# Router scores by GpSimd products and halving sums, and the choice of experts one sequence into the next tile

## The chip, the cores and the metric

The kernel runs on one core of a Trainium2 chip. A core has a matrix engine (TensorE, PE in the profile), VectorE (DVE), ScalarE (ACT), GpSimd (POOL), a queue engine that only issues transfers (SyncE, SP) and 16 DMA engines. Each engine works through its own queue in order and waits there for what its next instruction needs. The metric is the device time of one launch in microseconds (us), median of several runs; lower is better.

## The reference

One transformer block in float32: `x` is 64 sequences of 32 tokens of width 256, and each sequence has a context of 257 rows of width 128.

```python
x = x + cross_attention(layernorm(x), ctx)      # 16 heads of 64, keys and values from ctx
x = x + self_attention(layernorm(x))            # 4 heads of 64, half of each head with rotary angles
x = x + mixture_of_experts(layernorm(x))        # 8 experts, 2 per token
```

The part that matters here is the router of the last line. With `x` now the normed rows and `Wr` of 8 x 256:

```python
scores = einsum('bsd,nd->bsn', x, Wr) + br                 # 8 numbers per token
w      = softmax(scores)
_, idx = top_k(scores + biases_N, 2)                       # two experts per token
val    = take_along_axis(w, idx); val = val / val.sum(-1)
```

Each expert is `silu(x@Wl1_a + bl1_a) * (x@Wl1_b + bl1_b)`, 256 to 512, followed by `@ Wl2 + bl2`, 512 to 256; a token's two results are added with the weights `val`.

## The kernel before

**Tiles.** The 2048 tokens are 16 tiles `t` of 128 tokens, four sequences `b` each. The main loop (L1037) runs over the 64 pairs `(t, b)`. A pass of it transposes the probabilities of sequence `(t, b)` on PE (`probs_transposed`, tile `tp`, L338), mixes the context with them (`cross_mix`, `pa`, L348), and meanwhile forms the scores of the *next* sequence (`cross_probs`: `s` on PE L315, the negated maximum `nmx` on VectorE L319, the exponential on ScalarE L320, `inv` on VectorE L325, and the scaling `pr` of the four groups of 128 rows in two pairs, VectorE L327). So the second L327 pair of one pass is what the third and fourth `tp` transpose of the next pass need.

**Work beside it.** All else of the attention part is in Python generators that the loop advances a unit at a time, by the table `steps` (L932): one row per sequence of an even and an odd tile, six places in a row. `"near"` is the generator `rest(t)` (L557) of the tile before the loop's own, `"far"` that of the tile two before, `"ahead"` the cross-attention queries of the next pair of tiles (`cross_queries`, L250), which start at the end of each odd tile. `rest(t)` has 13 units: the cross-attention's output and a layer norm (3), self-attention (7, the rotary products L407 to L412 among them), and from unit 11 on `route(t, xr)` (L475): unit 11 transposes the normed rows `xr` (`trr`, PE, copied by ScalarE to `xrT`); unit 12 multiplies `xrT` with `Wr` (`pr`, L483, a 128x8 result) and chooses the experts with a dozen small VectorE instructions (`rsc` L485 to `xr` L522); unit 13 turns the choice into row numbers (`pk` on PE L527, `rat` to `rslots`, `seen`) and writes the rows to the expert lists in DRAM with two indirect transfers from the POOL queue (`routed`, L539). `carry` (L555) is a POOL instruction that hands the counts to the next tile. A tile takes 6 near and 7 far units, so its two experts are chosen in the third row (`b` = 2) and its rows written in the fourth row of the far tile.

**Layer norms.** `normed` (L173) takes statistics on VectorE, one power (`rstd`, L183) on POOL, and the scaling on VectorE (L186); its results are `xns`, `xr` and `xnq`. VectorE stands in its queue while POOL makes the power.

**Who sets the order.** PE and SP issue in the order of the program (`manual_schedule`, L79). ScalarE, VectorE and POOL are put in an order by a planner, which moves an instruction ahead of others where its estimates let it; `cross_queries`, traced at the end of an odd tile, has its two norms run two sequences earlier. `tc.keep_in_program_order(i)` holds `i` behind the instruction that was traced last on its engine, and behind that one alone.

**The expert part.** At the start of tile 15 `early_blocks` (L760) counts the lists up to the last tile that has been routed and prepares 6 blocks of 128 rows; after the loop these and the blocks of `late_blocks` run, 28 of them in the profiled execution, PE-bound, with weights streamed by SP.

**Queues.** SP issues every load in program order: the first loads end with `bn_bc` (L155), then come the zeros for `routed` (L1014), the context of tile 1 and so on. POOL's queue holds the powers, two additions `xb` and `axb` of 128x256 per tile (L356, L467), `carried`, the `routed` transfers, and in the expert part the adding transfers to the output.

Of the kernel before, what the change touches and what calls it, by code (L numbers as in the profile page):

```python
# [9 lines left out]
FP = mybir.dt.float32  # L10
# [6 lines left out]
P = 128  # L17
# [33 lines left out]
def block_kernel(  # L51
# [13 lines left out]
    awo: bass.AP,  # L65
    abo: bass.AP,
    freq: bass.AP,
    wr_t: bass.AP,
    br: bass.AP,
    bias_n: bass.AP,  # L70
# [38 lines left out]
    def pool(name, bufs):  # L109
        return ctx.enter_context(tc.tile_pool(name=name, bufs=bufs))  # L110
# [55 lines left out]
    sm = pool("sm", 4)  # L166
    xp = pool("xp", 3)
    tb = pool("tb", 1)

    def bank(shape, name):  # L170
        return ps.tile([P] + shape, FP, tag="a", name=name)
# [17 lines left out]
    def transposed(dst, src, n, name, beside=False):  # L189


        if beside:
            pt = ps.tile([P, n, P], FP, tag="t", bufs=2, name=f"tr{name}")
        else:
            pt = bank([n, P], f"tr{name}")
        for k in range(n):
            nc.tensor.transpose(pt[:, k, :], src[:, k * P : (k + 1) * P], ident)
        nc.scalar.copy(dst, pt)  # L198
# [276 lines left out]
    def route(t, xr):  # L475

        nc.gpsimd.tensor_copy(xr[:, RW - 1 : RW], token[:, t : t + 1])
        xT = wk.tile([P, 2, P], FP, tag="xrT", name=f"xrT{t}")
        transposed(xT, xr, 2, f"r{t}", t < NT - 2)
        yield  # L480
        pr = bank([NE], f"pr{t}")
        for k in range(2):
            nc.tensor.matmul(pr, xT[:, k, :], wr_sb[:, k, :], start=(k == 0), stop=(k == 1))  # L483
        sc = sm.tile([P, NE], FP, tag="rsc", name=f"rsc{t}")
        nc.vector.tensor_tensor(sc, pr, br_bc, ALU.add)  # L485
        sel = sm.tile([P, NE], FP, tag="rsel", name=f"rsel{t}")
        nc.vector.tensor_tensor(sel, sc, bn_bc, ALU.add)
        top = sm.tile([P, 8], FP, tag="rtop", name=f"rtop{t}")
        nc.vector.max(top, sel)
        idx = sm.tile([P, 8], U32, tag="ridx", name=f"ridx{t}")  # L490
        nc.vector.max_index(idx, top, sel)
        idf = sm.tile([P, 2, 1], FP, tag="ridf", name=f"ridf{t}")
        nc.vector.tensor_copy(idf[:, :, 0], idx[:, 0:2])

        two = sm.tile([P, 2, NE], FP, tag="rtwo", name=f"rtwo{t}")
        nc.vector.tensor_tensor(
            two, expert_id2, idf.to_broadcast([P, 2, NE]), ALU.is_equal
        )
        both = sm.tile([P, NE], FP, tag="rboth", name=f"rboth{t}")
        nc.vector.tensor_tensor(both, two[:, 0, :], two[:, 1, :], ALU.add)  # L500
        boths[t] = both
        if t < NT - 2:


            fed = sm.tile([P, NE], FP, tag="rfed", name=f"rfed{t}")
            nc.vector.scalar_tensor_tensor(fed, both, not_last, carried[t], ALU.mult, ALU.add)
        nmx = sm.tile([P, 1], FP, tag="rnmx", name=f"rnmx{t}")
        nc.vector.tensor_reduce(nmx, sc, AX.X, ALU.max, negate=True)
        ex = sm.tile([P, NE], FP, tag="rex", name=f"rex{t}")
        if t < NT - 2:  # L510
            nc.scalar.activation(ex, sc, AF.Exp, bias=nmx)
        else:

            nc.vector.tensor_scalar(ex, sc, nmx, None, ALU.add)
            nc.gpsimd.tensor_tensor(ex, euler, ex, ALU.pow)
        nc.vector.tensor_tensor(ex, ex, both, ALU.mult)
        tot = sm.tile([P, 1], FP, tag="rtot", name=f"rtot{t}")
        nc.vector.tensor_reduce(tot, ex, AX.X, ALU.add)
        inv = sm.tile([P, 1], FP, tag="rinv", name=f"rinv{t}")
        nc.vector.reciprocal(inv, tot)  # L520
        ew = xr[:, D : D + NE]
        nc.vector.tensor_scalar(ew, ex, inv, None, ALU.mult)  # L522
        yield

        pk = bank([NE], f"pk{t}")
        if t < NT - 2:
            nc.tensor.matmul(pk, before_all, fed, start=True, stop=True)  # L527
        else:
            nc.tensor.matmul(pk, before, both, start=True, stop=False)
            nc.tensor.matmul(pk, of_last, seen[t - 1], start=False, stop=True)  # L530
        at = sm.tile([P, 1, NE], FP, tag="rat", name=f"rat{t}")
        nc.vector.tensor_tensor(at[:, 0, :], pk, region[:, 0, :], ALU.add)
        nc.vector.tensor_tensor(two, two, at.to_broadcast([P, 2, NE]), ALU.mult)
        slot = sm.tile([P, 2], FP, tag="rslot", name=f"rslot{t}")
        nc.vector.tensor_reduce(slot, two, AX.X, ALU.add)
        slots = sm.tile([P, 2], U32, tag="rslots", name=f"rslots{t}")
        nc.vector.tensor_copy(slots, slot)
        for k in range(2):
            nc.gpsimd.indirect_dma_start(  # L539
                out=routed[:, :],  # L540
                out_offset=bass.IndirectOffsetOnAxis(ap=slots[:, k : k + 1], axis=0),
                in_=xr,
                in_offset=None,
            )
        if t >= NT - 2:

            nc.gpsimd.dma_start(out=out[t * P : (t + 1) * P, :], in_=xs[t])
        if t < NT - 1:
            seen[t] = sm.tile([P, NE], FP, tag="seen", name=f"seen{t}")
            nc.vector.tensor_tensor(seen[t], pk, both, ALU.add)  # L550
            carry(t)
# [308 lines left out]
    def rotary_tables():  # L860
# [69 lines left out]


    steps = (  # L932
        ("", "far", "ahead", "near", "far", ""),
        ("near", "far", "", "near", "far", ""),
        ("ahead", "far", "ahead", "near", "far", "ahead"),
        ("near", "", "ahead", "near", "", "far"),
        ("", "far", "ahead", "near", "far", ""),
        ("near", "far", "", "near", "far", ""),
        ("ahead", "far", "ahead", "near", "far", "ahead"),
        ("", "", "near", "near", "", "far"),  # L940
    )
    last_steps = steps[4:6] + (
        ("", "", "far", "near", "", "far"),
# [1 line left out]
    )  # L945
    kvs, probs = {0: context0}, {}
    seqs = [(t, b) for t in range(NT) for b in range(4)]
    work = {"near": last_rows(), "far": iter(()), "ahead": cross_queries(0)}
    next(work["ahead"])

    diag = [const.tile([P, AH, P], FP, name=f"diag{i}") for i in range(2)]
# [85 lines left out]
    for n, (t, b) in enumerate(seqs):  # L1037
        if n == 1:
            work["ahead"] = cross_queries(1)
            next(work["ahead"])  # L1040
        if n == 2:
            next(work["ahead"])
        if n == 3:
            load(base, freq.partition_broadcast(P))
        if n == 5:
            rotary_tables()
        if t == NT - 1 and b == 0:
            blocks, done = early_blocks()
            lane_of_queries(0)
        if b == 0:  # L1050
            cT = wk.tile([P, XH, 4, SEQ], FP, tag="cT", name=f"cT{t}")
            lastT = wk.tile([P, 4, SEQ], FP, tag="lastT", name=f"lastT{t}")
            if t + 1 < NT:
                kvs[t + 1] = load_context(t + 1)
            if t % 2 == 0 and t + 4 < NT:
                for j in (t + 4, t + 5):
                    load_tokens(j)
        place = iter(steps[4 * (t % 2) + b] if t < NT - 1 else last_steps[b])

        def step():  # L1060
            name = next(place)
            if name:
                next(work[name], None)

        scores = iter(())
        if n + 1 < len(seqs):
            t1, b1 = seqs[n + 1]
            scores = cross_probs(t1, b1, kvs[t1][0])
        pr, pts = probs.pop((t, b)), []
        probs_transposed(t, b, 0, pr, pts)  # L1070
        step()
        next(scores, None)
        next(scores, None)
        step()
        probs_transposed(t, b, 1, pr, pts)
        nc.vector.transpose(lastT[:, b, :], p_last[t % 2][b])
        next(scores, None)
        step()
        next(scores, None)
        step()  # L1080
        step()
        cross_mix(t, b, pts, kvs[t][1], cT)
        step()
        if t == NT - 1 and b == 1:
            load_last(t)
            blocks.weights(0, (0, 1), sure=True)
            for i in range(EARLY - 1):
                blocks.gathered(i)
        if b == 3:
            if t < NT - 1:  # L1090
                load_last(t)
            if t % 2:
                for _ in work["ahead"]:
                    pass
                if t + 3 < NT:
                    work["ahead"] = cross_queries((t + 3) // 2)
                    next(work["ahead"])
            for _ in work["far"]:
                pass
            work["far"] = work["near"]  # L1100
            work["near"] = rest(t, cT, lastT, u_ring[t % 3])

# [144 lines left out]
```

## Time and profile before

| | |
|---|---|
| median of 3 runs | 801.58 us (800.68 to 804.30) |
| the profiled execution's own time | 802.53 us |
| its span in the trace | 800.8 us |
| attention part | from 0 to about 600 us |
| one tile of it in the steady state | about 36 us (the router transposes of tiles 5 and 7 start at 291.1 and 363.2 us) |
| busy: PE, VectorE, ScalarE, POOL | 96%, 63%, 46%, 19% |
| POOL additions of 128x256 (`axb`), one | 724 / 726 / 743 ns (min / median / max) |
| `pr` scaling L327, one | 334 / 350 / 834 ns |

The profile page gives busy times and groups; the trace behind it can be asked for a stretch of time ("timeline": start, duration, engine, line, operation, out<-in, count, and in brackets the idle time before it and what ended it), for sums over stretches ("windows": for each engine busy time and number of instructions, then granted PE clock, DMA share and GB/s), and for who waited for whom. 1.00 is the full granted clock of PE. In the timeline, neighbours of the same kind are merged; a matrix product in float32 counts as two PE instructions, a transpose as one. Durations on an engine can overlap, so the distance from start to start is what an instruction takes away from its engine.

### The profile page before, as it was taken

Reading aid. Unit: us, or ns where it says so; the run is one execution under the profiler, and the core shown is the slowest. Engines: PE = TensorE matmul, PEld = TensorE weight load, DVE = VectorE, ACT = ScalarE, POOL = GpSimd, SP = SyncE. Lnnn points to the kernel's source line nnn. Section 1 sums busy time; section 2 is a strip of 40 time slices with the busy share of each in tenths; the row PEclk is TensorE's granted clock in tenths of the full one; section 3 lists DMA queues with packets and bytes.
Section 4 is the critical chain, followed back from the end, with each engine's and each line's share of the span. In section 5 each row is a group of like instructions: output and inputs, shape, how many; then the busy total and the mean of one; then the engine's idle time right before and its main releaser. Section 6 shows DMA issues by size and latency. Waiting matters only on the chain. (4 is left out here: it accounts for less than half of the span.)

```text
span 800.8 us, 15293 instructions
## 1 busy us (share of the span) xinstructions
PE 771.7 (96%) x5146; PEld 604.5 (75%) x5146; DVE 503.1 (63%) x2084; ACT 365.3 (46%) x1052; POOL 152.4 (19%) x214
## 2 busy tenths in 40 slices
PE   8899999999999999999999999999999899999994
PEld 7576677677767777777767777676678799999994
DVE  4657666766686676677677766768665633554442
ACT  3564555555465555546554555555434222212220
POOL 3001011120211111111111111121124412332332
PEclk9999999999999999999999999999999999999997
DMA  9440102021120202021110202020351396458432
GB/s 309 142 111 2 67 11 68 11 89 27 53 73 18 67 11 80 11 69 50 50 60 18 68 11 67 10 78 15 119 203 34 80 398 180 54 110 251 58 45 28
DMA packets 44258, 64.17 MB, mean 80 GB/s; under 512 B 19408, under 2 KB 35152, under 8 KB 42640
## 3 DMA queue, kind: packets, MB, share of 16 engines
q1 hardware_dynamic: 37648, 54.08, 20.8%
q0 software_dynamic: 6528, 9.06, 6.2%
q8 instruction: 43, 0.70, 0.4%
q14 instruction: 39, 0.32, 0.1%
HBM read 87.54 MB, written 13.16 MB: 126 GB/s over the span
## 5 line engine op out<-in xcount | busy, mean ns | idle before, releaser
L320 ACT ACTIVATE pr<-s,nmx 128x257 f32<-128x257 f32 x256 | 122.2, 481 | 111.8 <-DVE nmx L319 100.5
L319 DVE TENSOR_REDUCE nmx<-s 128x1 f32<-128x257 f32 x256 | 105.4, 420 | 71.0 <-PE s L315 70.4
L315 PE MATMUL s<-kv,q 128*128 128x257 f32 x512 | 143.1, 388 | 1.9 <-ACT pr L320 1.9
L348 PE MATMUL pa<-pt,kv 128*128 128x512 f32 x256 | 123.2, 604 | 5.0 <-ACT ov L372 4.9
L315 PEld LDWEIGHTS s<-kv,q 128*128 128x128 f32 x512 | 89.3, 193 | 16.7 <-ACT pr L320 3.2
L338 PEld LDWEIGHTS tp<-ident,pr 128*128 128x128 f32 x512 | 61.8, 144 | 30.6 <-issue 15.7
L338 PE MATMUL tp<-ident,pr 128*128 128x128 f32 x512 | 80.5, 279 | 1.6 <-DVE pr L327 1.6
L327 DVE TENSOR_SCALAR pr<-pr,inv 128x256 f32<-128x256 f32 x256 | 79.7, 353 | 3.4
L351 ACT COPY cT<-pa 128x512 f32<-128x512 f32 x64 | 37.5, 586 | 91.4 <-PE pa L348 91.4
L342 ACT COPY pt<-tp 128x512 f32<-128x512 f32 x128 | 75.6, 591 | 4.5 <-PE tp L338 3.5
L348 PEld LDWEIGHTS pa<-pt,kv 128*128 128x128 f32 x256 | 46.1, 190 | 39.4 <-issue 26.6
L752 POOL DMA_INDIRECT out_x<-y_late,to_late x28 | 43.5, 1555 | 104.0 <-DMA out_x<-y_late,to_late 39.0
L291 PE MATMUL pqh<-xqT,xwq_sb 128*128 128x256 f32 x256 | 60.8, 381 | 0.8 <-ACT xqT L198 0.8
L381 PE MATMUL po<-xwo_sb,ov 128*128 128x256 f32 x256 | 60.6, 379 | 0.0
L381 PEld LDWEIGHTS po<-xwo_sb,ov 128*128 128x128 f32 x256 | 48.6, 190 | 6.6
L291 PEld LDWEIGHTS pqh<-xqT,xwq_sb 128*128 128x128 f32 x256 | 47.3, 190 | 7.9 <-ACT xqT L198 1.5
L320 ACT ACTIVATION_READ_ACCUMULATOR pr<-s,nmx 128x1 f32 x256 | 52.1, 203 | 0.0
L325 DVE RECIPROCAL inv<-sums 128x2 f32<-128x2 f32 x128 | 20.8, 162 | 46.7 <-ACT pr L320 45.8
L728 ACT ACTIVATE sa_late<-pa_late,lane 128x128 f32<-128x128 f32 x72 | 20.6, 369 | 63.6 <-PE pa_late L712 63.6
L555 POOL TENSOR_SCALAR carried<-seen,is_last 128x8 f32<-128x8 f32 x15 | 5.3, 353 | 218.6 <-DVE seen L550 218.6
L539 POOL DMA_INDIRECT routed<-xr,rslots x32 | 33.0, 1032 | 59.2 <-DMA routed<-xr,rslots 22.0
L396 PE MATMUL pqkv<-awqkv_sb,xaT 128*128 128x512 f32 (+1 forms) x128 | 43.9, 486 | 0.0
(275 smaller groups left out, 1270.8 us busy)
## 6 DMA issues: line engine op xcount, KB each, us to landing
lane<-in_wall SPq DMA_DIRECT2D x24, 1028.0 KB
lane<-in_wall SPq DMA_DIRECT2D x24, 640.0 KB
lane2a<-in_wall SPq DMA_DIRECT2D x10, 1028.0 KB
kv<-in_ctx_t SPq DMA_DIRECT2D x16, 514.0 KB
kv<-in_ctx_a SPq DMA_DIRECT2D x16, 512.0 KB
lane2b<-in_wall SPq DMA_DIRECT2D x10, 640.0 KB
xg_late<-routed SPq DMA_DIRECT2D x80, 32.0 KB
x<-in_x SPq DMA_DIRECT2D x16, 128.0 KB
```

The lines of the kernel that those rows point to most:

```text
L291: nc.tensor.matmul(pq[:, mm, :], xwq_sb[:, k, m * P : (m + 1) * P], xqT[:, k, :], start=(k == 0), stop=(k == 1),)
L315: nc.tensor.matmul(s, qb[:, g * P : (g + 1) * P], kvT[:, b, :], start=True, stop=True)
L319: nc.vector.tensor_reduce(nmx, s, AX.X, ALU.max, negate=True)
L320: nc.scalar.activation(pr[:, g, :], s, AF.Exp, bias=nmx, accum_out=sums[:, g : g + 1])
L327: nc.vector.tensor_scalar(pr[:, i, :ML], pr[:, i, :ML], inv[:, i : i + 1], None, ALU.mult)
L338: nc.tensor.transpose(tp[:, g * P : (g + 1) * P], pr[:, g, j * P : (j + 1) * P], ident)
L342: nc.scalar.copy(pt, tp)
L348: nc.tensor.matmul(pa, kvA[:, b, j, :], pts[j], start=(j == 0), stop=(j == MC - 1))
L351: nc.scalar.copy(cT[:, :, b, :], pa.rearrange("p (h n) -> p h n", n=SEQ))
L381: nc.tensor.matmul(po, ov[:, m, :], xwo_sb[:, m, :], start=False, stop=(m == XH // 2 - 1))
L396: nc.tensor.matmul(pq, xaT[:, k, :], awqkv_sb[:, k, lo:hi], start=(k == 0), stop=(k == 1))
L752: nc.gpsimd.indirect_dma_start(out=out[:, :], out_offset=bass.IndirectOffsetOnAxis(ap=self.to[:, b : b + 1], axis=0), in_=y, in_offset=Non ...
```

## The change

For the first 13 tiles (`t < NT - 3`) the router's scores no longer come from PE. Unit 11 now issues 20 POOL instructions: for each of four pairs of experts two products of `xr` with a row of `Wr` that has been broadcast to 128 partitions (128x256 each), and three additions that halve the length, from 2x256 to 2x32. Unit 12 starts with one VectorE sum of 128x8x32 to 128x8 (`sums`), which is held by `keep_in_program_order`, and goes on as before. The last three tiles keep the PE form. The eight rows of `Wr` are loaded at the start, behind `bn_bc`, into tiles whose places the expert part uses later; the products use the place of `v_last`. In the table of steps units 12 and 13 move to a new generator slot `"late"`, served at the first and the last place of `b` = 0 of the tile after the far one; the four rows of odd tiles change in the same places.

```diff
+    wr_rows = []
+    for e in range(NE):
+        tag, bufs = (("y", 4), ("bxT", 2), ("wr_row", 2))[(e > 3) + (e > 5)]
+        wr_rows.append(xp.tile([P, D], FP, tag=tag, bufs=bufs, name=f"wr_row{e}"))
+        load(wr_rows[e], wr[e, :].partition_broadcast(P))
...
     def route(t, xr):
         nc.gpsimd.tensor_copy(xr[:, RW - 1 : RW], token[:, t : t + 1])
-        xT = wk.tile([P, 2, P], FP, tag="xrT", name=f"xrT{t}")
-        transposed(xT, xr, 2, f"r{t}", t < NT - 2)
-        yield
-        pr = bank([NE], f"pr{t}")
-        for k in range(2):
-            nc.tensor.matmul(pr, xT[:, k, :], wr_sb[:, k, :], start=(k == 0), stop=(k == 1))
         sc = sm.tile([P, NE], FP, tag="rsc", name=f"rsc{t}")
-        nc.vector.tensor_tensor(sc, pr, br_bc, ALU.add)
+        if t < NT - 3:
+            part = wk.tile([P, NE, SEQ], FP, tag="rpart", bufs=1, name=f"rpart{t}")
+            for e in range(0, NE, 2):
+                prod = wk.tile([P, 2, D], FP, tag="v_last", bufs=1, name=f"rprod{t}_{e}")
+                for i in range(2):
+                    nc.gpsimd.tensor_tensor(prod[:, i, :], xr[:, 0:D], wr_rows[e + i], ALU.mult)
+                n = D // 2
+                while n >= SEQ:
+                    dst = prod[:, :, :n] if n > SEQ else part[:, e : e + 2, :]
+                    nc.gpsimd.tensor_tensor(dst, prod[:, :, :n], prod[:, :, n : 2 * n], ALU.add)
+                    n //= 2
+            yield
+            sums = sm.tile([P, NE], FP, tag="rsums", name=f"rsums{t}")
+            tc.keep_in_program_order(nc.vector.tensor_reduce(sums, part, AX.X, ALU.add))
+            nc.vector.tensor_tensor(sc, sums, br_bc, ALU.add)
+        else:
+            xT = wk.tile([P, 2, P], FP, tag="xaT", name=f"xrT{t}")
+            transposed(xT, xr, 2, f"r{t}", t < NT - 2)
+            yield
+            pr = bank([NE], f"pr{t}")
...
+            nc.vector.tensor_tensor(sc, pr, br_bc, ALU.add)
...
     steps = (
-        ("", "far", "ahead", "near", "far", ""),
+        ("late", "far", "ahead", "near", "far", "late"),
         ("near", "far", "", "near", "far", ""),
-        ("ahead", "far", "ahead", "near", "far", "ahead"),
-        ("near", "", "ahead", "near", "", "far"),
+        ("ahead", "far", "ahead", "near", "", "ahead"),
+        ("near", "", "ahead", "near", "", ""),
...
-            for _ in work["far"]:
+            for _ in work["late"]:
                 pass
+            work["late"] = work["far"]
             work["far"] = work["near"]
             work["near"] = rest(t, cT, lastT, u_ring[t % 3])
```

More of the change, by code (lines that the diff above doesn't have):

```diff
@@ L67, in block_kernel @@
     freq: bass.AP,
+    wr: bass.AP,
     wr_t: bass.AP,
@@ L477, in route @@
         nc.gpsimd.tensor_copy(xr[:, RW - 1 : RW], token[:, t : t + 1])
-        xT = wk.tile([P, 2, P], FP, tag="xrT", name=f"xrT{t}")
-        transposed(xT, xr, 2, f"r{t}", t < NT - 2)
-        yield
-        pr = bank([NE], f"pr{t}")
-        for k in range(2):
-            nc.tensor.matmul(pr, xT[:, k, :], wr_sb[:, k, :], start=(k == 0), stop=(k == 1))
-        sc = sm.tile([P, NE], FP, tag="rsc", name=f"rsc{t}")
-        nc.vector.tensor_tensor(sc, pr, br_bc, ALU.add)
+        sc = sm.tile([P, NE], FP, tag="rsc", name=f"rsc{t}")
+        if t < NT - 3:
[18 more added lines that the diff above has]
+            pr = bank([NE], f"pr{t}")
+            for k in range(2):
+                nc.tensor.matmul(
+                    pr, xT[:, k, :], wr_sb[:, k, :], start=(k == 0), stop=(k == 1)
+                )
+            nc.vector.tensor_tensor(sc, pr, br_bc, ALU.add)
         sel = sm.tile([P, NE], FP, tag="rsel", name=f"rsel{t}")
@@ L932, in block_kernel @@
     steps = (
-        ("", "far", "ahead", "near", "far", ""),
+        ("late", "far", "ahead", "near", "far", "late"),
         ("near", "far", "", "near", "far", ""),
-        ("ahead", "far", "ahead", "near", "far", "ahead"),
-        ("near", "", "ahead", "near", "", "far"),
-        ("", "far", "ahead", "near", "far", ""),
+        ("ahead", "far", "ahead", "near", "", "ahead"),
+        ("near", "", "ahead", "near", "", ""),
+        ("late", "far", "ahead", "near", "far", "late"),
         ("near", "far", "", "near", "far", ""),
-        ("ahead", "far", "ahead", "near", "far", "ahead"),
-        ("", "", "near", "near", "", "far"),
+        ("ahead", "far", "ahead", "near", "", "ahead"),
+        ("", "", "near", "near", "", ""),
     )
@@ L947, in block_kernel @@
     seqs = [(t, b) for t in range(NT) for b in range(4)]
-    work = {"near": last_rows(), "far": iter(()), "ahead": cross_queries(0)}
+    work = {"near": last_rows(), "far": iter(()), "late": iter(()), "ahead": cross_queries(0)}
     next(work["ahead"])
@@ L1222 @@
         "freq": a["L0_attn_nrope_freq"],
+        "wr": a["L0_ffn_Wr"],
         "wr_t": a["L0_ffn_Wr"].T,
```

## The prediction

> **What bounds the kernel now.** I read the page's busy line, then the stretches of the attention part, then the timeline of one tile.
>
> ```profile
> PE 771.7 (96%) x5146; PEld 604.5 (75%) x5146; DVE 503.1 (63%) x2084; ACT 365.3 (46%) x1052; POOL 152.4 (19%) x214
> 285.00:320.00 35.00, 34.63 (x228) 25.11 (x227) 25.66 (x108) 19.54 (x58) 6.09 (x10) 1.00 0.16 52
> 320.00:355.00 35.00, 34.63 (x227) 25.21 (x226) 22.97 (x94) 18.17 (x51) 5.03 (x8) 1.00 0.14 45
> ```
>
> PE is busy 34.63 of each 35.00 us at the full clock: about 0.6 us of PE work removed from a tile is 0.6 us won, and any wait of PE is lost in full. POOL is nearly idle, but VectorE is the engine that feeds PE's next transposes. That feeding is what the change touches, as a tile with an odd number shows (tile 5; start, duration, engine).
>
> ```profile
> 290.34 0.41 DVE L186 TENSOR_SCALAR xr<-x,mvr,rstdr 128x256 f32<-128x256 f32 x1 [0.50 <-POOL rstdr L183]
> 291.11 0.38 PE L197 MATMUL trr<-ident,xr 128*128 128x128 f32 x2
> 291.33 0.60 PE L338 MATMUL tp<-ident,pr 128*128 128x128 f32 x4
> 291.48 0.55 POOL L183 TENSOR_TENSOR rstdq<-veq,minus_half 128x1 f32<-128x1 f32 x1 [0.52 <-DVE veq L181]
> 294.11 0.51 PE L483 MATMUL pr<-wr_sb,xrT 128*128 128x8 f32 x4
> 294.48 1.98 PE L348 MATMUL pa<-pt,kv 128*128 128x512 f32 x4
> ...
> 294.75 0.40 DVE L186 TENSOR_SCALAR xnq<-x,mvq,rstdq 128x256 f32<-128x256 f32 x1
> 295.39 0.17 DVE L325 RECIPROCAL inv<-sums 128x2 f32<-128x2 f32 x1
> 295.62 0.60 DVE L327 TENSOR_SCALAR pr<-pr,inv 128x256 f32<-128x256 f32 x2
> 297.46 0.66 PE L338 MATMUL tp<-ident,pr 128*128 128x128 f32 x4
> ```
>
> The normed router rows `xr` are ready at 290.75; the second L327 pair runs at 295.62 and PE takes it at 297.46, 1.2 us after it ends. Tiles 1, 3, 7 and 9 repeat this to 0.01 us (6.71 us from `xr` to that `tp`). The next tile is looser: `xr` at 324.97, last rotary product ended at 342.56.
>
> **What it removes.** Start to start, `trr` takes 291.33 - 291.11 = 0.22 us of PE, `pr` 294.48 - 294.11 = 0.37: 0.59 us per tile, 13 x 0.59 = 7.7 us if PE stays full. The copy `xrT` (0.37 us) goes from ScalarE, which is 46% busy and not the bound: nothing.
>
> **What it adds on POOL.** Per tile 12 instructions of 256 elements, 4 of 128, 4 of 64. The row for 256 is `axb`, 0.73 us, 0.68 start to start when the next is independent. The short ones are not in the trace; the line through the 128x1 copy (0.19) and `axb` gives 0.45 and 0.32. Sum 12 x 0.73 + 4 x 0.45 + 4 x 0.32 = 11.8 us. From below, time in proportion to elements: 12 x 0.68 + 4 x 0.34 + 4 x 0.17 = 10.2. From above, no two-input instruction cheaper than the 128x1 power (0.55): 13.2, and 0.1 for each of 15 waits of an addition for the one before it (VectorE to POOL is 0.09 at `ver` to `rstdr`): 14.7. I take 11.8 with 0.05 a wait. All of it lies beside PE; what counts is who waits for its end.
>
> **The added wait.** `sums` stands in VectorE's queue and waits for the last of the 20. It is traced at the start of the next tile, some 15 us after `xr`, but `keep_in_program_order` holds it only behind the VectorE instruction traced last. After an even tile that is a rotary product of the last row: fine. After an odd tile it is the second `xnq` of `cross_queries`, which the planner runs two sequences early. VectorE's order in the built program of the changed kernel, for such a tile:
>
> ```
> L194 xr_4430
> ...
> L327 nmx_3_3_4523
> L194 xnq_4636
> L502 rsums_4654<-rpart_4475
> L333 inv_3_4458
> L503 rsc_4474
> L335 pr_3_4459 x2
> ```
>
> This is so in five tiles, 1, 3, 5, 7, 9; in the other eight `sums` comes 30 instructions or more behind `xr`. Queued behind `sums` in the five are `inv`, the second `pr` pair (waited for by `tp` on PE), the choice of experts and all `nmx` of the next sequence.
>
> *The five tiles*, on tile 5's clock. POOL starts at 290.83. Two products end at 292.24; the second `rstdq` stands next in its queue (+0.50); three additions with waits, 1.65, to 294.4. Three more pairs at 1.41 + 1.70 = 3.1 each: 303.7; 0.6 us while VectorE still holds SBUF (below): 304.3. Then `sums` (0.34 start to start, as `nmx`), `inv` 0.20, `rsc` 0.10, the first `pr` 0.35: 305.3. PE has done the two transposes of the first pair by then and wants the third, which stood at 297.46 + 0.22 = 297.68. Delay 7.6 us; the 0.59 us saved lies before the wait and is swallowed. With POOL's bounds 4.9 to 9.9. Five tiles: **+38 us** (25 to 50). Nothing makes it up, since PE was the bound on both sides.
>
> *The clock.* Before, PE idled 1.57 us at 22.55 in a thin stretch, and the records show:
>
> ```profile
> 24.13 0.56 PE L338 MATMUL tp<-ident,pr 128*128 128x128 f32 x2 [1.57 <-DVE pr L327]
> 24.52 1.86 PE L315 MATMUL s<-kv,q 128*128 128x257 f32 x4
> 20.00:24.58 4.58, 2.96 (x15) 1.74 (x16) 3.17 (x9) 1.72 (x5) 0.00 (x0) 1.00 0.62 191
> 24.58:28.00 3.42, 3.42 (x12) 2.76 (x12) 0.85 (x2) 2.19 (x6) 0.00 (x0) 0.50 0.82 215
> 28.00:31.40 3.40, 3.40 (x22) 2.69 (x21) 2.96 (x13) 1.61 (x5) 0.04 (x1) 1.00 0.90 291
> ```
>
> For 3.42 us the clock was 0.50, and four `s` took 1.86 instead of the 1.03 us of tile 5; 3.42 x (1 - 1.03/1.86) = 1.5 us lost. An idle time of 8 us is longer than that stretch, so I expect half clock behind each of the five: one stretch on average and a part of a second, 1.9 us (0 to 3.0). Five: **+9.5 us** (0 to 15).
>
> [...]
>
> *The other eight tiles.* PE saves 8 x 0.59 = **-4.7 us**. Their 20 POOL instructions run 14.6 us (11.8, waits 0.75, VectorE's holds 2.0), to 339.6 in tile 6, against 342.56 less a little: `sums` finds its input ready with 2 to 3 us to spare (tile 11: 506.43 to 521.89, 0.9 us). But the engines collide. One L327 of 256 fell into an `axb`:
>
> ```profile
> L327 DVE TENSOR_SCALAR pr<-pr,inv x256: 334/350/834, 19.4 to 577.1; 128x256 f32<-128x256 f32 x128
> 71.63 1.09 DVE L327 TENSOR_SCALAR pr<-pr,inv 128x256 f32<-128x256 f32 x2
> 71.85 0.72 POOL L467 TENSOR_TENSOR axb<-x,abo_bc 128x256 f32<-128x256 f32 x1 [6.28 <-issue]
> ```
>
> It took 0.834 instead of 0.350 us and ended with the addition. Three L327 pairs and two rotary products fall into a tile's products: at most 8 x 0.48 = 3.9 us of VectorE time, in a stretch where VectorE idles 5.8 us, so 0.3 us of PE per tile (0 to 1.2). A dozen small instructions moved into the busier first sequence: 0.3 (0 to 1), as VectorE idles 1.2 us there and 2.1 just after. Eight tiles: **+4.8 us** (0 to 18).
>
> [...]
>
> **The rest.** `pk`, `carried` and the two `routed` transfers come one sequence later; POOL's second one must await the first (3 to 7 us between them before) and is then close ahead of the next `xb`, `axb` and `rstds`: +0.5 (0 to 5). `early_blocks` counts to tile 11 instead of 12, so PE's wait for `seen` goes (1.3 us in the list of PE's waits): -1.3. Eight broadcast loads of 128 KB, 1 MB at the 309 GB/s of the page's first slice, are 3.4 us of transfers and 8 x 0.43 us of SP; behind them come the zeros for `routed` (18.2) and tile 1's context (26.0), first needed at 49.8: 0 (to 3.4). The expert part is the same.
>
> **Sum**, on the profiled execution (802.53, of which 800.8 is the span; 1 us above the median): 802.5 + 38 + 9.5 - 4.7 + 4.8 + 0.5 - 1.3 = 849.3; I say 849.
>
> **Rivals.** (1) *Faster.* If VectorE did not reach `sums` before its input is there, the removed PE work would stay: 802.5 - 7.7 - 1.3 = 793.5, or 798 with the collisions. It needs the products to end by about 297.7 in the odd tiles, 7 us after `xr`; twelve instructions of 0.68 us alone take 8.2. Only a POOL twice as fast on these forms does it. (2) *The waits without the clock*: the idle time falls so that PE keeps 1.00: 840. Against it, 1.57 us were enough at 22.55. (3) *All thirteen wait*: POOL at its upper bound, with collisions, ends after the rotary products in the other eight as well, by 0.5 to 2 us each, and the five wait 9.9: 802.5 + 50 + 9.5 + 10 = 872. (4) *Nothing*: five waits of 1.2 us would eat the gain; that needs the products to end by 299.
>
> **Chances.** Forecast 0.58, (2) 0.16, (3) 0.21, (1) 0.04, (4) 0.01. Range 828 (short POOL, little clock loss: 802.5 + 25 + 5 - 4.7) to 873. About 0.5% (4 us) is what a measurement of this kernel tells from no change: faster 0.04, same 0.01, slower 0.95.
>
> **What would show it.** Right: in five tiles VectorE idle before the `sums` line on POOL for 8 to 10 us, PE idle before `tp` on `pr` about 8 us each, 40 in all, half clock behind it; POOL about 12 us of additions and products a tile; L327's maximum and mean up; no wait at `sums` in even tiles. Wrong: short instructions far from 0.45 and 0.32 us; waits in even tiles; a clock that stays at 1.00.

## The result, and the profile after

The changed kernel takes 853.67 us (median of 5 runs, 851.22 to 856.89) against 802.20 us for the kernel before on the same chip (5 runs, 800.68 to 806.91): ratio 1.063, 95% interval 1.058 to 1.067. The profiled execution took 851.84 us, its span is 849.5 us. On the profiled executions the prediction was +46.8 us; it is +49.3.

The busy line of the page of the changed kernel:

```profile
PE 777.3 (92%) x5068; PEld 604.3 (71%) x5068; DVE 519.3 (61%) x2097; ACT 360.6 (42%) x1039; POOL 305.3 (36%) x474
```

PE has 78 instructions fewer than before, six for each of the thirteen tiles, but its share fell from 96% to 92%: it now idles. The list of waits of the changed kernel (engine, waiting instruction, what released it; us in total, number, longest) says for whom:

```profile
DVE rsums L502 <- POOL rpart L498: 43.8, 5, 8.8
PE tp L346 <- DVE pr L335: 42.9, 9, 8.1
```

VectorE stands before `sums` five times, and PE before the transposes of `pr`. The timeline of the changed kernel in tile 5 (start, duration, engine; VectorE's lines, then PE's, then POOL's last) shows the chain that the prediction built:

```profile
306.27 0.41 DVE L194 TENSOR_SCALAR xr<-x,mvr,rstdr 128x256 f32<-128x256 f32 x1 [0.50 <-POOL rstdr L191]
306.79 0.94 DVE L194 TENSOR_SCALAR xnq<-x,mvq,rstdq 128x256 f32<-128x256 f32 x1
309.48 0.82 DVE L335 TENSOR_SCALAR pr<-pr,inv 128x256 f32<-128x256 f32 x2
311.15 0.40 DVE L194 TENSOR_SCALAR xnq<-x,mvq,rstdq 128x256 f32<-128x256 f32 x1
320.31 0.42 DVE L502 TENSOR_REDUCE rsums<-rpart 128x8 f32<-128x256 f32 x1 [8.76 <-POOL rpart L498]
320.65 0.15 DVE L333 RECIPROCAL inv<-sums 128x2 f32<-128x2 f32 x1
320.85 0.61 DVE L335 TENSOR_SCALAR pr<-pr,inv 128x256 f32<-128x256 f32 x2
...
312.77 0.44 PE L346 MATMUL tp<-ident,pr 128*128 128x128 f32 x2
321.25 0.80 PE L346 MATMUL tp<-ident,pr 128*128 128x128 f32 x2 [8.05 <-DVE pr L335]
321.85 1.92 PE L323 MATMUL s<-kv,q 128*128 128x257 f32 x4
...
319.96 0.32 POOL L498 TENSOR_TENSOR rpart<-rprod 128x64 f32<-128x64 f32 x1
```

Right behind the second `xnq` stands `sums`, for 8.76 us, until POOL's last addition; the second `pr` pair is behind it, and PE does two transposes and then idles 8.05 us for the third. Before, the second pair of this place ran at 295.62 and PE took it, right behind the first, without idling (the line at 297.46 holds both). PE's third `tp` comes 14.56 us after the end of `xr` (306.69). Before, it started at 297.73 (the third of the four in that line), 6.98 us after `xr`: it is 7.58 us later. The four `s` behind the wait take 1.92 us, at half clock. The windows of the same place (length, then busy us of PE, PEld, VectorE, ScalarE and POOL, granted clock, DMA share, GB/s):

```profile
285.00:316.20 31.20, 27.85 (x197) 19.91 (x195) 21.33 (x91) 15.32 (x43) 14.18 (x23) 1.00 0.16 50
316.20:326.40 10.20, 5.15 (x14) 3.83 (x15) 5.15 (x27) 3.03 (x10) 3.66 (x7) 0.50 0.00 1
326.40:355.00 28.60, 28.23 (x191) 21.33 (x191) 19.02 (x73) 14.31 (x43) 8.61 (x14) 1.00 0.19 63
```

The half clock lasts 10.24 us in the records, half of it in the idle time and half behind it. All five idle times are 8.04 to 8.06 us long; the first brought a stretch of 6.83 us, the other four 10.24. POOL's own rows, by form:

```profile
L494 POOL TENSOR_TENSOR rprod<-xr,wr_row 128x256 f32<-128x256 f32 x104 | 74.7, 738 | 6.4 <-DVE xr L194 2.8 <-PE pqh L299 0.5
L498 POOL TENSOR_TENSOR rprod<-rprod 128x256 f32<-128x256 f32 x52 | 38.1, 732 | 3.7
L498 POOL TENSOR_TENSOR rprod<-rprod 128x128 f32<-128x128 f32 x52 | 24.1, 464 | 4.1
L498 POOL TENSOR_TENSOR rpart<-rprod 128x64 f32<-128x64 f32 x52 | 16.7, 321 | 4.1
```

A measure used from here on is the time from the end of one tile's `xr` to the end of the next one's, minus the same in the kernel before (us, one profiled execution each; the step from an odd tile to the next holds that odd tile's products and the wait at its `sums`):

```
kernel        start to 0  0 to 1  odd to next (five)  even to next (five)  11 to 12  12 to 13  13 to end   span
changed         -1.81     -0.58   +9.38 to +10.25     -0.49 to -0.44        0.00     +0.37     +3.26      +48.8
hold            -2.38     -0.58   +0.24 to +0.26      -0.47 to -0.43       -0.01     +0.99     +4.02       +1.1
longer          -1.72     -0.34   +12.66 to +13.07    +0.16 to +0.20       +1.03     +1.69     +3.81      +70.1
filler          -1.43     -0.58   +8.72 to +8.75      -0.48 to -0.38       -0.04     +0.37     +1.17      +41.0
steps_only      -1.90     +0.92   -0.13 to +0.08      +0.15 to +0.16       +0.17     -0.51     +6.11       +5.7
unread          -1.91     -0.06   +1.64 to +1.66      +1.52 to +1.99       +0.04     +1.79     +0.35      +16.9
unread_late     -2.43     +0.09   +0.43 to +0.44      +0.20 to +0.23       +0.58     +1.29     +5.12       +7.9
hold_12         -2.08     -0.57   +0.24 to +0.25      -0.47 to -0.42       -0.02      0.00     +3.39       -0.2
even_only       -2.07     -0.59   +0.04 to +0.05      -0.58 to -0.50       +0.05     +0.01     +1.32       -3.8
```

So five steps carry the loss: 9.38 + 9.86 + 10.12 + 10.20 + 10.25 = 49.8 us. The first column is not the change's: the profiled execution of the kernel before had the half-clock stretch at 24.58 to 28.00 that the prediction showed, and none of the nine others has one there. The column behind tile 13 has such chance in it too: in the expert part the profiled execution of steps_only was at half clock for 6.83 us from 639.6 on (it took 808.21 us, where the kernel's ten executions took 802.86 to 808.93), those of changed, hold, longer and unread_late for 3.41 us each, the others not at all.

### The profile page after: what moved, and what is told of

Its sections match the earlier page's. It is cut to its first block, busy times and chain, and to the rows that moved or that the text cites. A ratio compares the mean times of both kernels' runs of the same rounds, so it can differ in the third digit from the quotient of the medians.

```text
span 849.5 us, 15385 instructions
## 1 busy us (share of the span) xinstructions
PE 777.3 (92%) x5068; PEld 604.3 (71%) x5068; DVE 519.3 (61%) x2097; ACT 360.6 (42%) x1039; POOL 305.3 (36%) x474
## 2 busy tenths in 40 slices
DMA packets 45985, 68.62 MB, mean 81 GB/s; under 512 B 19600, under 2 KB 36368, under 8 KB 44112
## 5 line engine op out<-in xcount | busy, mean ns | idle before, releaser
L323 PE MATMUL s<-kv,q 128*128 128x257 f32 x512 | 148.7, 400 | 3.2 <-ACT pr L328 1.9
L327 DVE TENSOR_REDUCE nmx<-s 128x1 f32<-128x257 f32 x256 | 103.9, 419 | 49.6 <-PE s L323 48.8
L346 PE MATMUL tp<-ident,pr 128*128 128x128 f32 x512 | 88.3, 288 | 43.4 <-DVE pr L335 42.9
L346 PEld LDWEIGHTS tp<-ident,pr 128*128 128x128 f32 x512 | 65.0, 147 | 78.4 <-DVE pr L335 41.7
L323 PEld LDWEIGHTS s<-kv,q 128*128 128x128 f32 x512 | 92.4, 200 | 18.9 <-ACT pr L328 8.5
L335 DVE TENSOR_SCALAR pr<-pr,inv 128x256 f32<-128x256 f32 x256 | 88.6, 385 | 3.8
L494 POOL TENSOR_TENSOR rprod<-xr,wr_row 128x256 f32<-128x256 f32 x104 | 74.7, 738 | 6.4 <-DVE xr L194 2.8
L498 POOL TENSOR_TENSOR rprod<-rprod 128x256 f32<-128x256 f32 x104 | 62.2, 598 | 7.8
```

The costliest lines, as they stand in the source:

```text
L323: nc.tensor.matmul(s, qb[:, g * P : (g + 1) * P], kvT[:, b, :], start=True, stop=True)
L327: nc.vector.tensor_reduce(nmx, s, AX.X, ALU.max, negate=True)
L335: nc.vector.tensor_scalar(pr[:, i, :ML], pr[:, i, :ML], inv[:, i : i + 1], None, ALU.mult)
L346: nc.tensor.transpose(tp[:, g * P : (g + 1) * P], pr[:, g, j * P : (j + 1) * P], ident)
L494: nc.gpsimd.tensor_tensor(prod[:, i, :], xr[:, 0:D], wr_rows[e + i], ALU.mult)
L498: nc.gpsimd.tensor_tensor(dst, prod[:, :, :n], prod[:, :, n : 2 * n], ALU.add)
```

## Experiments

Theory: `sums` is held in the wrong place after odd tiles, VectorE waits for POOL there, and half clock comes on top. Rivals: POOL's products cost that much by themselves, beside VectorE; or the table of steps does.

### The same kernel with `sums` held behind the last rotary product (hold)

```diff
+        rotary[0] = nc.vector.tensor_tensor(x2, x2, x1s, ALU.add)
...
-            tc.keep_in_program_order(nc.vector.tensor_reduce(sums, part, AX.X, ALU.add))
+            with tc.issue_after(rotary[0].ins):
+                nc.vector.tensor_reduce(sums, part, AX.X, ALU.add)
```

> The changed kernel with one edit: `sums` is held behind the last rotary product of the row before (in odd tiles too) and not behind the second xnq. Theory: the place of `sums` in VectorE's queue in five odd tiles is the whole loss. Then the five idle times of 8.8 us before `sums` go, PE keeps 1.00 through the attention part, each odd tile saves about 0.45 us like the even ones, and the span falls by 49.8 + 2.3 us to about 797; time 799 to 802, ratio to before 0.994 to 1.000. Rival: POOL's 13 us per tile beside VectorE cost the time (blocked scalings, moved choice of experts). Then the time stays over 830.

Measured: 804.04 us against 802.89, ratio 1.0023 (1.0010 to 1.0036). From the timeline of this kernel in the place of tile 5 (VectorE, then POOL):

```profile
286.98 0.41 DVE L194 TENSOR_SCALAR xr<-x,mvr,rstdr 128x256 f32<-128x256 f32 x1 [0.50 <-POOL rstdr L191]
302.31 0.41 DVE L505 TENSOR_REDUCE rsums<-rpart 128x8 f32<-128x256 f32 x1
...
300.92 0.32 POOL L500 TENSOR_TENSOR rpart<-rprod 128x64 f32<-128x64 f32 x1
```

POOL's last addition again ends 13.9 us after `xr`, but `sums` now stands 14.9 us behind it and does not wait. The same products, loads and steps run, and 49.6 of the 51 us are gone: the place of one VectorE instruction was the loss, all but 1 to 2 us. The gain that was expected of the removed PE work is not there either, though. An even tile's step is 0.45 us shorter, an odd one's 0.25 us *longer*, so there 0.59 + 0.25 = 0.84 us are lost; and the part behind tile 13 is 4 us longer. The moved steps alone cost an odd step at most 0.08 us (steps_only). PE idles 0.43 us more in the step of tile 5, 0.24 before `tp` and 0.19 before `pov`; the rest was not taken apart.

### POOL's work lengthened (longer)

```diff
-                for i in range(2):
+                for i in (0, 0, 1):
                     nc.gpsimd.tensor_tensor(prod[:, i, :], xr[:, 0:D], wr_rows[e + i], ALU.mult)
```

> The changed kernel with one of the eight products of POOL made twice in each pair of experts, four more instructions of 0.73 us per tile, 2.9 us. Theory (VectorE stands for POOL's products in the five tiles behind an odd one, and in the other eight there are 2 to 4 us to spare): the wait at the sum grows from 8.8 to 11.7 us in five tiles and appears in one more by at most 1 us; 866 to 872 us. Rival A (products cost PE in all tiles, by collisions): about 0.4 us more in each of thirteen tiles beside it, 872 to 880. Rival B (the wait is not for POOL's length but for a place in the order): as the changed kernel, 850 to 857.

Measured: 872.54 us, ratio 1.0858 (1.0831 to 1.0886). The wait list and the timeline of this kernel in tile 5:

```profile
DVE rsums L502 <- POOL rpart L498: 54.2, 5, 10.8
...
331.85 0.80 PE L346 MATMUL tp<-ident,pr 128*128 128x128 f32 x2 [10.72 <-DVE pr L335]
```

Still five waits; no sixth appeared. PE's wait grew by 2.67 us, close to the 2.9 us of added POOL work (VectorE's own by 2.0, since it came 0.8 us later). The five odd steps took 64.65 us in place of 49.8, +14.8: this is the theory's term. But the even steps grew too, by about 0.65 us each, and the steps of 0, 11 and 12 by 0.24, 1.03 and 1.32: 5.8 us without any wait at `sums`, as rival A had it (it said 0.4 each). So both are shown; the total lies between them. Why the last 2.9 us of POOL work cost an even tile five times what the first 13 us did, the trace tells in part. Behind tile 6 a scaling pair `pr` that ran just after POOL's products in the changed kernel (364.18, 0.62 us) now falls beside them (375.32) and takes 1.41 us; the `nmx`, the exponential and the copy `cT` behind it are late, and PE idles 0.50 us before `tp` for `cT`. PE has five such waits, 2.5 us in all; the changed kernel has one, of 0.3.

### PE kept busy in the wait (filler)

```diff
+        if b == 3 and t % 2 == 1 and 3 <= t <= 11:
+            filler = bank([4 * P], f"filler{t}")
+            for _ in range(9):
+                nc.tensor.matmul(filler, ident, xwv_sb[:, : 4 * P], start=True, stop=True)
```

> The changed kernel with nine products of 128x512 on PE, whose results nobody reads, ahead of the third transpose of tiles 3, 5, 7, 9 and 11 of the loop, that is in the five waits. PE then works for about 7.7 of the 8 us in which it idled. Theory (part of the loss is the half clock behind the idle time): the stretches of 10.24 us at half clock behind the waits go, and with them about 2.3 us per wait, so that an odd tile costs +7.8 us in place of +10.2: 840 to 845 us. Rival (the clock lost nothing that counts): 850 to 857 us, as the changed kernel.

Measured: 843.74 us, ratio 1.0518 (1.0492 to 1.0545). PE's timeline in tile 5's wait:

```profile
311.46 7.99 PE L1101 MATMUL filler<-xwv_sb,ident 128*128 128x512 f32 x18
319.29 0.38 PE L346 MATMUL tp<-ident,pr 128*128 128x128 f32 x2
319.99 0.59 PE L346 MATMUL tp<-ident,pr 128*128 128x128 f32 x2 [0.32 <-DVE pr L335]
320.42 1.03 PE L323 MATMUL s<-kv,q 128*128 128x257 f32 x4
```

The edit puts the products ahead of the first two transposes of that pass, so these now come behind them. The products fill the wait to 0.32 us, the four `s` take 1.03 us again, and no half clock is left in the records but the one at the kernel's end. The odd steps fall to 8.73 us each: 49.8 - 43.7 = 6.1 us are gone with the half clock and are put down to it, 1.2 us per wait on average (0.65 to 1.5), not the 2.3 expected. Small waits of PE for VectorE, which is late with all it has queued behind `sums`, now show in tile 5: 0.32 us before `tp`, 0.34 before `pqkv` and 0.29 before the next pass's `tp`. The slow work had covered them: the changed kernel has none of them behind its wait. Behind the changed kernel's wait in tile 5 lay 5.2 us at half clock, where four `s` took 1.92 us in place of 1.03; an estimate from these is 5.2 x (1 - 1.03/1.92) = 2.4 us lost. The run shows 1.2 per wait. Without the half clock the last two of the small waits cost 0.63 again; the rest of the difference was not taken apart. The half-clock stretches of these kernels, those at their ends apart, are 3.41, 6.83, 10.24 and 13.65 us long (the last in the kernel with longer products): one to four times 3.41.

### The table of steps alone (steps_only)

The kernel before with the new slot `"late"` and the changed table, the router on PE, no rows loaded and no products.

```diff
-        ("", "far", "ahead", "near", "far", ""),
+        ("late", "far", "ahead", "near", "far", "late"),
...
-            for _ in work["far"]:
+            for _ in work["late"]:
                 pass
+            work["late"] = work["far"]
```

> The changed table of steps and the late slot alone: the router stays on PE in all tiles, no products on POOL, no rows of Wr loaded. Theory: the attention part is that of before within 2 us, and the expert part is longer by 3 to 4 us with 3.4 MB more traffic: 803 to 807. Rival: moving the choice of experts into the first sequence costs PE time by itself (up to 1 us a tile): 810 to 818.

Measured: 806.17 us, ratio 1.0033 (1.0013 to 1.0053). The moved steps cost 0.15 us in an even step and at most 0.08 in an odd one. In the profiled execution 6.1 us come behind tile 13, 2.4 of them behind the first late block, where its half clock lies. That part was costed in the prediction as unchanged but for -0.8, and is taken up below.

### Products that nobody reads (unread, unread_late)

The kernel before, with the rows loaded and POOL's 20 instructions per tile issued in unit 11, but the router left on PE:

```diff
+        if t < NT - 3:
+            part = wk.tile([P, NE, SEQ], FP, tag="rpart", bufs=1, name=f"rpart{t}")
+            for e in range(0, NE, 2):
+                prod = wk.tile([P, 2, D], FP, tag="v_last", bufs=1, name=f"rprod{t}_{e}")
+                for i in range(2):
+                    nc.gpsimd.tensor_tensor(prod[:, i, :], xr[:, 0:D], wr_rows[e + i], ALU.mult)
...
         xT = wk.tile([P, 2, P], FP, tag="xaT", name=f"xrT{t}")
         transposed(xT, xr, 2, f"r{t}", t < NT - 2)
```

> The kernel before with the 20 POOL instructions added in the first 13 tiles, their results read by nobody; the router stays on PE, the steps are those of before. It measures the cost of POOL's work beside VectorE by itself. Theory: the even tiles of the changed kernel lost 0.13 us of their 0.59 us, so 13 tiles cost about 2 us: 803 to 806, with L327's maximum near 0.9 us and its mean near 0.385 us. Rival, blocking for whole runs of POOL instructions: 8 to 18 us more, 810 to 820.

Measured: 820.70 us, ratio 1.0251 (1.0218 to 1.0284). The theory (803 to 806) missed, and the time is just above the rival's 810 to 820. Nobody waits for these products, and still they cost 1.5 to 2.0 us per tile from tile 1 to 11. PE's waits in this kernel:

```profile
PE pqkv L403 <- DVE q L290: 5.9, 5, 1.2
PE tp L345 <- DVE pr L334: 5.2, 7, 1.6
PE pa L355 <- DVE q L290: 3.3, 5, 0.7
```

PE waits for VectorE, and VectorE's rows by form say what is late there. First the kernel before, then this one:

```profile
L500 DVE TENSOR_TENSOR rboth<-rtwo 128x8 f32<-128x8 f32 x16 | 2.3, 145 | 0.3
L506 DVE SCALAR_TENSOR_TENSOR rfed<-rboth,not_last,carried 128x8 f32<-128x8 f32 x14 | 3.2, 227 | 0.5
L518 DVE TENSOR_REDUCE rtot<-rex 128x1 f32<-128x8 f32 x16 | 2.6, 161 | 0.6
```

```profile
L518 DVE TENSOR_TENSOR rboth<-rtwo 128x8 f32<-128x8 f32 x16 | 7.1, 441 | 0.3
L524 DVE SCALAR_TENSOR_TENSOR rfed<-rboth,not_last,carried 128x8 f32<-128x8 f32 x14 | 7.4, 527 | 0.5
L536 DVE TENSOR_REDUCE rtot<-rex 128x1 f32<-128x8 f32 x16 | 2.6, 161 | 0.6
```

An addition of 8 numbers a partition takes 441 ns in place of 145 on average. The timeline of tile 5 (VectorE, then POOL) shows what it waits for:

```profile
302.83 0.58 DVE L518 TENSOR_TENSOR rboth<-rtwo 128x8 f32<-128x8 f32 x1
303.44 0.65 DVE L524 SCALAR_TENSOR_TENSOR rfed<-rboth,not_last,carried 128x8 f32<-128x8 f32 x1
304.20 0.16 DVE L536 TENSOR_REDUCE rtot<-rex 128x1 f32<-128x8 f32 x1
...
302.63 1.44 POOL L490 TENSOR_TENSOR rprod<-xr,wr_row 128x256 f32<-128x256 f32 x2
304.15 1.26 POOL L494 TENSOR_TENSOR rprod<-rprod 128x256 f32<-128x256 f32 x2
```

POOL's first product ends at 303.39 and `rboth` at 303.41; the second ends at 304.07 and `rfed` at 304.09. Four of this chain (`rboth`, `rfed`, `rsel`, the scaling into `xr`) gained 0.89 us per tile together, while the sum `rtot`, beside one of POOL's additions here, kept its 161 ns. The scaling into `xr` (230 to 400 ns) reads one tile of 128x8 and a number per partition, the other three have two inputs of 8 numbers; what decides which instruction is struck, no run shows.

These instructions are struck because they lie beside the products there; in the changed kernel the table of steps takes them to the next tile. So the same products were run with that table (the edit of steps_only on top of this one):

> Products that nobody reads, beside the router on PE, as in the run before, but with the table of steps of the changed kernel, so that the choice of experts stands one sequence into the next tile, behind the products. Theory (the products cost 1.5 to 2 us per tile there because the small instructions of the choice, one after the other, fell into them: the sum of two halves took 441 ns in place of 145): 806 (steps alone) plus 0.2 to 0.8 us per tile, 808 to 815 us. Rival (products of POOL cost that much wherever the choice stands): 819 to 826 us.

Measured: 810.45 us, ratio 1.0090 (1.0064 to 1.0117). The same two rows of this kernel:

```profile
L518 DVE TENSOR_TENSOR rboth<-rtwo 128x8 f32<-128x8 f32 x16 | 2.7, 167 | 0.5
L524 DVE SCALAR_TENSOR_TENSOR rfed<-rboth,not_last,carried 128x8 f32<-128x8 f32 x14 | 3.0, 216 | 0.0
```

The chain is fast again, and a tile costs 0.2 to 0.44 us in place of 1.5 to 2.0. VectorE's long instructions are struck as before (`pr` has a mean of 398 ns here, 402 there, 353 without products), so they alone do not cost PE the 1.2 to 1.5 us. For the even tiles the chain of small ones is shown as the cause: in tile 6 of the run before, the copy `q` stands on VectorE right behind the chain (341.88), and PE idles 1.20 us for it before `pqkv` (the first of the three waits above). For the odd tiles it is so only in part. Of the two waits there, the one of 0.67 us before `pa` (the third line) ends at 300.10, ahead of the chain, and follows an `xnq` of 0.95 us and a `pr` pair of 0.94. It went with the new table as well, which also takes the router's product out of PE's queue just ahead of that `pa`; the two were not separated. This also says what the moved choice is good for.

### Tile 12 back on PE (hold_12)

Behind tile 13 the changed kernel's PE has two waits that were not there before, or only for 0.6 us (the second):

```profile
PE pa_early L740 <- DMA lane<-in_wall: 2.7, 2, 1.7
PE pxT_late L707 <- DMA xg_late<-routed: 2.2, 2, 1.9
```

The lists of experts are counted one tile earlier now (`early_blocks`, up to tile 11). Worked out from the router's choices for these inputs (no run prints these counts), full blocks of 128 rows up to tile 12 are 3 3 3 3 3 3 2 3 for the eight experts, up to tile 11 they are 2 3 2 3 2 3 2 2. The six early blocks are then of experts 0 0 1 1 1 2 in place of 0 0 0 1 1 1. The first three of the six use one buffer for weights (`lane`), the other three a second one, and the two take turns. Before, neither had to be filled again within the six; now both have to, for the fifth and the sixth block that run. The trace fits: PE's two waits for `lane` are at these two blocks (669.54 and 676.83), and from 663.93 to 683.96 DMA moved 230 GB/s where before, from 618.45 to 637.66, it moved 65, which is 3.4 MB more, two times the 1.7 MB of one expert. Traffic is 68.62 MB in place of 64.17 in all, of which the eight rows are 1.05. To test it, the held kernel with tile 12 routed by PE, within tile 14, so that the lists are counted as before:

```diff
-        if t < NT - 3:
+        if t < NT - 4:
...
+    tile14_steps = steps[0:2] + (
+        ("ahead", "far", "ahead", "near", "far", "ahead"),
+        ("near", "", "ahead", "near", "", "far"),
+    )
```

> As hold, but tile 12 keeps the router on PE and is routed within tile 14, in the two places of the steps of before, so that the early blocks count to tile 12 again. Theory: the changed kernel's expert part is 3.6 us longer because with counts to tile 11 the blocks fall to the experts in another way (3.4 MB more weights are moved, PE waits 2.7 us for a lane and 2.2 us for rows). Then DMA traffic falls from 68.6 MB to about 65.2 MB, these waits go, and the time is 3 us under hold's: 796 to 798.5. Rival: the waits come from the rows of the last tiles being written later, or from the run: then the traffic or the waits stay and the time is hold's.

Measured: 802.42 us, ratio 0.9998 (0.9985 to 1.0011). The traffic is 65.21 MB, the wait for `lane` is gone, and `pxT_late` waits 0.7 us as before (0.6). From the first `pa_early` to the first `pxT_late` the changed kernel took 2.0 us more than before, hold 2.9, steps_only 3.7; hold_12 0.6, unread (lists as before) 0.0. The other kernels fall in with this: counted to tile 11, longer 2.5, filler 1.4, unread_late 2.4; counted to tile 12, even_only -0.1. So the earlier count is shown as the cause there. The time is only 1.6 us under hold's, though, not 3. hold_12 is still 3.4 us longer behind tile 13, 1.9 of it after PE's last product; that was not explained.

### POOL's scores for even tiles only (even_only)

```diff
-        if t < NT - 4:
+        if t < NT - 4 and t % 2 == 0:
```

and the last two rows of the table as they were in the kernel before.

> The held kernel without tile 12, with POOL's scores only for the even tiles 0 to 10; odd tiles keep the router on PE and the old places of the steps. Theory (an even tile gains 0.45 us, an odd one loses 0.25 by collisions): the odd tiles come back to 0 to +0.1 us, six even ones gain 2.7 us, so 798.5 to 801.5 us, ratio 0.996 to 0.999. Rival (the gain of an even tile is only work moved into the odd one behind it): ratio 0.999 to 1.003.

Measured: 800.14 us (12 runs, 797.96 to 802.92) against 802.78 (17 runs), ratio 0.9969 (0.9951 to 0.9987). The odd steps are back to +0.05 us, the even ones gain 0.50 to 0.58, nearly all of the 0.59 us that PE is spared, and among PE's waits the longest are those of the kernel before:

```profile
PE tp L346 <- DVE pr L335: 1.6, 1, 1.6
PE py_early L776 <- DVE g_early L764: 1.5, 2, 1.3
PE pc_early L606 <- DVE seen L581: 1.3, 1, 1.3
```

This version is 0.3% faster than the kernel before. The idea of the change holds in the even tiles, where POOL's products cost PE next to nothing (unread_late less steps_only: 0.06 us a step, against 0.36 in an odd one) and nobody waits for them. What in the odd tiles makes the difference was not separated.

## Why the prediction was right, and where it was not

**The five waits (+38).** Right in place, number and size. The prediction had POOL's last addition 13.55 us after `xr` and PE's third `tp` 14.55 us after it; they are 13.59 and 14.56. The delay of that transpose is 7.58 us (7.6), five times 37.9. That POOL's end fits to 0.04 us is in part luck: an addition waits 0.08 us for the one before it (0.80 from start to start where one takes 0.72), not 0.05, which adds about 0.4 us. The 0.6 us for VectorE holding POOL is shown by no run; in its place the trace of tile 5 has about 0.3, as two pairs of POOL's products and a pair of additions took 1.48, 1.51 and 1.34 us beside VectorE's work, where such pairs took 1.40 and 1.25 while VectorE stood. The two short forms, which no row of before had, were put at 0.45 and 0.32 us by a line through two rows, and are 0.464 and 0.321. That the held kernel takes 804 us shows that nothing else makes more than 1 to 2 us of the loss.

**The clock (+9.5).** Right in sign and in its range, 6.1 us measured with the filler. The price per wait (1.9) was too high, though the length was right: one stretch of 3.42 us and a part of a second were expected behind the wait, and behind it lay 5.2 us at half clock in tile 5 (321.25 to 326.42), but 1.2 us were won back without it, in part because PE would have waited for VectorE anyway. What was missing is that backlog: VectorE's work queued behind `sums` delays PE after the transpose. What is left of the odd steps is 49.8 - 37.9 - 6.1 = 5.8 us, or 1.2 per tile; of this the filler's trace of tile 5 shows 0.63 as the two small waits behind the transpose, and the rest was not taken apart. Together the two terms are 11.9 for the 9.5.

**The other eight tiles (-4.7 + 4.8 = +0.1).** Measured -0.58 - 2.29 + 0.00 + 0.37 = -2.5. No wait at `sums` in any of them, as said. The mis-sized term is collisions and moved instructions, put at 0.3 us each per tile: an even step lost 0.59 - 0.46 = 0.13, and the table of steps alone costs an even step 0.15, so the collisions cost PE nothing that shows there. The size would have been nearer for the odd tiles (0.84 in the held kernel, 0.44 for products and steps with nobody waiting), where the forecast had it swallowed. VectorE is held by POOL as predicted: the second `xnq` row above takes 0.94 us beside POOL's first products (the one at 311.15 takes 0.40), and the scaling's mean rose from 353 to 385 ns. "VectorE's holds" of POOL, 2.0 us in these tiles, are shown by no run: POOL's last addition ends 13.02 us after `xr` in tile 6 where 14.6 was forecast (the pairs of products took 1.41 to 1.46 us there, 1.40 in tile 5 while VectorE stood), and `sums` starts 3.9 us later, so there was more to spare than the 2 to 3 us said.

**The rest (+0.5 - 1.3, "the expert part is the same").** This step failed. Behind tile 13 it is +3.3 us: counting one tile less changed which experts the early blocks take, 2.0 us to the first late block with 3.4 MB more weights. PE's wait for `seen` went, as said, but what it won was lost again: it stood in the step from tile 12 to 13, and that step is 0.37 us longer all the same, as PE now waits there before `s` (0.86 us) and four times before `tp` (1.2 in all). The prediction priced the count by the wait that it removed and did not ask what the count decides. Another 1.3 us come after that; a half-clock stretch of 3.41 us begins at 684.8, and in the kernel with the filler, which has none there, these 1.3 us are gone. The two transfers `routed` (+0.5) have no row that prices them by themselves.

**The sum.** 38 + 9.5 + 0.1 - 0.8 = 46.8 stood against -1.8 (the start) + 49.8 - 2.5 + 3.3 = 48.8 of the span. The errors of the terms are up to 4 us and partly cancel: that the sum fits to 2 us is luck.

**Rivals.** (2) was the forecast without the clock loss, 840; the filler made that kernel, 843.7. (3) found no wait in even tiles even with 2.9 us more POOL work. (1) has its condition in the held kernel, where VectorE does not reach `sums` before its input; its price was too good: with no wait the kernel takes 804, not 793.5 to 798, since the odd tiles lose more than PE is spared, and the experts' part gives back the rest.

## What to carry to other kernels

Where a planner reorders, "behind what was traced last" is no place in time: look in the built order for what the held instruction stands behind on its queue, and count how long its input takes from there. Work that is moved to an idle engine is not free for its neighbours: ask what of VectorE's lies beside it, above all a chain of small instructions. Here `rboth` and `rfed` each ended 0.02 us behind one of POOL's products and took 0.58 and 0.65 us in place of 0.145 and 0.227. And a step that comes a tile later can change what is decided by it; follow the decision, not only the wait.

## What the hardware showed unexpectedly

- Twenty POOL instructions that nobody reads, 13 us of a 36 us tile, slowed the kernel by 2.5% as long as the choice of experts lay beside them, and 8-element VectorE instructions suffered most for their size: 145 to 441 ns and 227 to 527 ns, while the sums of 8 kept 161 ns.
- Idle times of PE of 8.04 to 8.06 us brought half-clock stretches of 10.24 us four times and 6.83 once, those of 10.7 us in the kernel with longer products 13.65 us; yet removing the first kind gave only 1.2 us back per wait.
- POOL's two-input additions in float32 took 732, 464 and 321 ns for 256, 128 and 64 elements; an estimate by a line through the three is a fixed part of about 0.2 us and 2.1 ns an element.
